# Attention scores and FFN on one core: five passes of scores a slot in place of six, with fill work between the runs and the product with v behind them

## The chip, the core and the metric

The kernel runs on one core of one Trainium2 chip. The metric is the device time of one execution in microseconds (us). The engines are named as in the profile: PE is TensorE's matmuls and PEld its weight loads, DVE is VectorE, ACT is ScalarE, POOL is GpSimd, SP is SyncE. "L515" is line 515 of the kernel before.

## What is computed

One transformer layer on x of shape 2 x 1024 x 512 (float32): a layer norm and attention of 32 heads of width 16, then a layer norm and a feed-forward part with quantised activations and weights (512 to 1376 to 512), each with a residual. The part that the change touches is the attention:

```python
q, k, v = (proj(w_q), proj(w_k), proj(w_v))          # 2 x 32 heads x 1024 x 16
scores = jnp.einsum('bhqd,bhkd->bhqk', q, k) / jnp.sqrt(jnp.float32(D_K))
attn = jax.nn.softmax(scores, axis=-1)
out = jnp.einsum('bhqk,bhkd->bhqd', attn, v)
```

## The kernel before

**Steps and slots.** The attention is cut into 32 steps. A step is one batch, one half of the queries (512), one group of 128 channels (8 heads) and half of its heads: 4 heads. Each of the 4 heads has its own 32 rows (partitions) of the tiles `kst` (keys) and `qst` (queries), so four matmuls with 32 rows each, one per head, can stand in TensorE side by side on four row groups. A step has 8 slots, one per 128 keys (for the exponentials) or per 128 queries and half of the keys (for the maxima). The main loop runs over slots, `T`, and in each slot three different steps are at work: the maxima of the step `nm`, the exponentials of an earlier step `ne` (10 slots behind), and the product with v of the slot before (`nw`).

**Two kinds of scores.** Scores are computed twice. For the maxima (`max_mm`, L475) queries are the stationary side; two passes `l` = 0, 1 (high and low parts of q) accumulate a 128 x 1024 tile `psm` for a pair of heads, and `max_reduce` (L485, DVE) takes the maximum of each row. At the end of a step `max_parts` (L490 to L493, DVE) joins these maxima, and one slot later `max_rows` (L498, PE; L502, ACT) transposes them into `mrow`. For the exponentials (`exp_mm`, L515) keys are the stationary side; two passes give the scores of a pair of heads and a third pass with ones adds the negative maximum from `mrow`; `exponentials` (L519, ACT) then reads this 128 x 1024 tile `pse` and writes `e`. `weigh_values` (L545, PE) multiplies `e` with v into `pso`, and after the last slot of a step copies the sum out (L554, ACT).

**Pairs.** A pair of heads takes two of the four row groups. So the exponentials of the pair 0 (`exps[0]`, row groups 0 and 1) are issued together with the maxima of the pair 1 (`maxs[0]`, row groups 2 and 3), and in the second run the other way round. I call the tiles e0 and m0 (first) and e1 and m1 (second). In a run before the change, `scores` issues e0 alone in the first pass, then e0 with m0, then e0's third pass with m0's second: three passes, of which the first uses two row groups. Two runs make six passes a slot.

**PSUM.** The score tiles `pse` and `psm`, and the transposed maxima `psn`, come from one pool `ps_s` of three buffers, two banks each. The product with v has one bank (`ps_a`), and all other work one bank (`ps_o`). A new tile waits until the reader of the tile that had its buffer is done: ACT for a `pse`, DVE for a `psm`.

**Fill work.** Projections, layer norms and the FFN are generators in the class `Fillers`. In a slot `fill.run(budget)` advances those that are ready until the PE time they name (`("pe", 860.0)`, in ns) reaches the budget: 1300 ns, or 1800 when a projection is near its due slot; what was overdrawn is taken from the next slot (`left`). `("gap", n)` lets a task rest for n calls. A task that needs PSUM asks for the bank with `("take",)`; a bank given back is free from the next call of `run` on. `run(100.0, short=True)` takes only short tasks (the transposes of FFN inputs L780 and of the hidden rows L863). Each call of `run` also advances the "back" tasks, which use no PE: the normalisation of the attention (L571 copy and L572 reciprocal on DVE, L582 on POOL, four DMAs) and the quantisation of the weights. When the loop ends, `turn` works off what is left.

**Order.** The schedule is written by hand: instructions stand in each engine's queue in the order in which the program issues them. In a slot of the kernel before, the order is: run A (e0, m0), product with v of the slot before, short fill, run B (e1, m1), fill. The exponential of a run stands in ACT's queue and the reduction in DVE's queue right behind the run's matmuls, ahead of what the fill issues next.

Of the kernel before, what the change touches and what calls it, by code (L numbers as in the profile page):

```python
# [148 lines left out]
def kernel(  # L149
# [50 lines left out]
    fill = Fillers()  # L200
# [43 lines left out]
    def scores_psum(name):  # L244
        return ps_s.tile([P, 2, QB], F32, tag="s", name=name)
# [201 lines left out]
    def load_k(n):  # L447
        kst[n] = sb.tile([P, S], F32R, tag="kst", name=f"kst_{n}", bufs=3)
        nc.sync.dma_start(kst[n].bitcast(F32), step_k(n))

    def load_q(n):
        b, h, g, s = steps[n]
        qst[n] = []
        for l in range(2):
            q = sb.tile([P, QB], F32R, tag="qst", name=f"qst_{n}_{l}", bufs=6)
            rows = qD[b, g, h][l].rearrange("(r s e) q -> s r e q", r=4, s=2)[s]
            nc.sync.dma_start(q.bitcast(F32), rows)
            qst[n].append(q)

    def load_v(n):  # L460
        b, h, g, s = steps[n]
        vt[n] = sb.tile([P, NT, 4, 32], F32, tag="v", name=f"v_{n}", bufs=2)
        nc.sync.dma_start(vt[n].rearrange("p t r e -> p (t r e)"), vD[b, g, s].rearrange("p t e -> p (t e)"))

    def max_tile(n, i, j):

        if i == 0 and n not in pm:
            pm[n] = sp.tile([P, TQ, 2, 4], F32, tag="pm", name=f"pm_{n}")
        return scores_psum(f"psm_{n}_{i}_{j}")

    def max_mm(n, i, j, ps, l):
        kh, t = divmod(i, TQ)
        for r in (2 * j, 2 * j + 1):
            rows = slice(32 * r, 32 * r + 32)
            nc.tensor.matmul(  # L475
                ps[:, r % 2, :],
                qst[n][l][rows, t * P : (t + 1) * P],
                kst[n][rows, kh * QB : (kh + 1) * QB],
                start=(l == 0),
                stop=(l == 1),  # L480
            )

    def max_reduce(n, i, j, ps):
        kh, t = divmod(i, TQ)
        nc.vector.tensor_reduce(pm[n][:, t, kh, 2 * j : 2 * j + 2], ps, AX.X, ALU.max, negate=True)  # L485

    def max_parts(n):
        m = sp.tile([P, TQ, 4], F32, tag="m", name=f"m_{n}")
        p = pm.pop(n)
        nc.vector.tensor_tensor(m, p[:, :, 0, :], p[:, :, 1, :], ALU.min)  # L490
        cols = mcols[n % 2].rearrange("p t (r c) -> p t r c", r=4)
        nc.vector.tensor_copy(cols[:, :, :, 0], m)
        nc.vector.tensor_tensor(cols[:, :, :, 1], m, cols[:, :, :, 0].bitcast(F32), ALU.subtract)  # L493

    def max_rows(n):
        ps = scores_psum(f"psn_{n}")[:, 0, :]
        for t in range(TQ):
            nc.tensor.matmul(  # L498
                ps[:, t * P : (t + 1) * P], mcols[n % 2][:, t, :], identr, start=True, stop=True
            )  # L500
        mrow[n] = sb.tile([P, QB], F32R, tag="mrow", name=f"mrow_{n}", bufs=2)
        nc.scalar.copy(mrow[n], ps)  # L502
# [3 lines left out]
    def exp_mm(n, i, j, ps, l):  # L506
        for r in (2 * j, 2 * j + 1):
            rows = slice(32 * r, 32 * r + 32)
            if l < 2:
                left, right = kst[n][rows, i * P : (i + 1) * P], qst[n][l][rows, :]  # L510
            else:

                rows = slice(32 * r, 32 * r + 2)
                left, right = onesr[rows, :], mrow[n][rows, :]
            nc.tensor.matmul(ps[:, r % 2, :], left, right, start=(l == 0), stop=(l == 2))  # L515

    def exponentials(n, i, j, ps):
        e = sb.tile([P, 2, QB], F32, tag="e", name=f"e_{n}_{i}_{j}", bufs=4)
        nc.scalar.activation(e, ps, AF.Exp, scale=SCALE)  # L519
        probs.setdefault((n, i), {})[j] = e  # L520

    def scores(exps, maxs):


        es = [(*x, scores_psum(f"pse_{x[0]}_{x[1]}_{x[2]}")) for x in exps]
        ms = [(*x, max_tile(*x)) for x in maxs]
        for l in range(3):
            for x in es:
                exp_mm(*x, l)
            if l or not es:  # L530
                for x in ms:
                    max_mm(*x, l - bool(es)) if l - bool(es) < 2 else None
        for x in es:
            exponentials(*x)
        for x in ms:
            max_reduce(*x)

    acc, po, OT = {}, {}, {}

    def weigh_values(n, i):  # L540
        if i == 0:
            acc[n] = ps_a.tile([P, QB], F32, tag="a", name=f"pso_{n}")
        e = probs.pop((n, i))
        for r in range(4):
            nc.tensor.matmul(  # L545
                acc[n][32 * r : 32 * r + 32, :],
                vt[n][:, i, r, :],
                e[r // 2][:, r % 2, :],
                start=(i == 0),
                stop=(i == NT - 1),  # L550
            )
        if i == NT - 1:
            po[n] = sb.tile([P, QB], F32, tag="po", name=f"po_{n}", bufs=3)
            nc.scalar.copy(po[n], acc[n])  # L554
# [340 lines left out]
    def now(gen):  # L895
        for _ in gen:
            pass
# [80 lines left out]
    NSTEP = len(steps)  # L978
# [23 lines left out]
    def feed():  # L1002

        while ffns and set(ffns[0][2]) <= fill.done | {ffns[0][2][0]}:
            name, gen, after, due = ffns.popleft()
            fill.add(name, gen, after, "ffn", due)


    SHARE, MORE = 1300.0, 1800.0
    left = 0.0  # L1010
    for T in range(LE + NT * NSTEP + 1):
        fill.slot = T
        ne, ie = divmod(T - LE, NT)
        nm, im = divmod(T, NT)
        nw, iw = divmod(T - LE - 1, NT)

        fill.scores = int(T < LE - 1 or T >= NT * NSTEP)

        if (T + 5) % NT == 0 and 1 < (T + 5) // NT < NSTEP:
            n = (T + 5) // NT  # L1020
            b, h, g, s = steps[n]
            fill.ensure(f"k_{b}_{g}_0", f"k_{b}_{g}_1", f"q_{b}_{g}_{h}")
            load_k(n)
            load_q(n)
        if (T - 8) % NT == 0 and 0 <= (T - 8) // NT < NSTEP:
            n = (T - 8) // NT
            b, h, g, s = steps[n]
            fill.ensure(f"v_{b}_{g}_0", f"v_{b}_{g}_1")
            load_v(n)
        if T in (TQ, NT):  # L1030
            fill.ensure(f"first_{T // NT}")
        if im == 0 and 0 < nm <= NSTEP:
            max_parts(nm - 1)
        exps = [(ne, ie, j) for j in range(2)] if 0 <= ne < NSTEP else []
        maxs = [(nm, im, j) for j in (1, 0)] if nm < NSTEP else []
        mixed = bool(exps and maxs)
        if mixed:
            scores(exps[:1], maxs[:1])
        elif exps:
            scores(exps, [])  # L1040
        if 0 <= nw < NSTEP:
            weigh_values(nw, iw)
            if iw == NT - 1 and nw % 2 and nw < NSTEP - 1:
                b, h, g, _ = steps[nw]
                fill.add(f"norm_{b}_{h}_{g}", normalise(nw), (), "back")
        feed()
        fill.run(100.0, short=True)
        if mixed:
            scores(exps[1:], maxs[1:])
        elif maxs:  # L1050
            scores([], maxs)
        if im == 1 and 0 < nm <= NSTEP:
            max_rows(nm - 1)
        share = MORE if fill.urgent() else SHARE
        left = fill.run(min(share + left, share))

    fill.scores = 3
    normalise_last(NSTEP - 1)
# [50 lines left out]
```

## Time and profile before

| | us |
|---|---|
| median of 3 runs | 1315.37 |
| lowest, highest | 1308.07, 1317.15 |
| the profiled execution | 1320.16 |
| its span | 1318.4 |

The span is the time from the first to the last instruction. The page of the profile lists busy time by engine, then groups of instructions by line with the mean of one in ns and the idle time ahead of them. PE's granted clock is 0.965 on the mean. By stretches of the run (us from the start; busy us of each engine):

| stretch | what runs there | PE | DVE | ACT | POOL |
|---|---|---|---|---|---|
| 0 to 121 | norms, first projections, first maxima | 82.7 | 47.8 | 26.1 | 26.2 |
| 121 to 350 | slots, projections, weight quantisation | 214.8 | 161.4 | 131.5 | 107.2 |
| 350 to 1190 | slots, projections, FFN | 823.4 | 603.4 | 500.0 | 111.9 |
| 1190 to 1222 | slots with exponentials alone | 30.2 | 4.5 | 21.9 | 1.3 |
| 1222 to 1318 | last FFN tiles | 58.3 | 49.4 | 32.6 | 0.0 |

An instruction of a group may be short and still decide: what counts is which wait ends last. Ends of matmuls in the profile are modelled, so their starts say more than their durations.

### The profile page before, as it was taken

To read this page: it belongs to the slowest core of one execution; us is meant where nothing else is said; L and a number is where in the kernel's file an instruction comes from. 1 tells how busy PE (TensorE), PEld (TensorE's weight loads), DVE (VectorE), ACT (ScalarE), POOL (GpSimd) and SP (SyncE) were. 2 spreads that over 40 slices of the span, in tenths; PEclk is the share of its full clock that TensorE was granted. 3 is DMA by queue.
4 is the path that set the end of the run, shared out by engine and by line. 5 is a ranking of instruction groups with operands and counts; after the bars stand their busy time and mean duration, and the time that the engine had idled before them with its cause. 6 is when DMAs were issued, how large, how long until landed. Compare 5 with 4: busy or idle time off the path is not lost.

```text
span 1318.4 us, 22143 instructions
## 1 busy us (share of the span) xinstructions
PE 1209.3 (92%) x9082; PEld 541.6 (41%) x9082; DVE 866.5 (66%) x1203; ACT 712.1 (54%) x903; POOL 246.5 (19%) x279
## 2 busy tenths in 40 slices
PE   5768899999999999999999999999999999999566
PEld 2345444334445443444444444444433344443222
DVE  6521468778865667687776676877776867772634
ACT  1124655545655555665666556666665556666243
POOL 1034326455511100321101003110010111100000
PEclk9889999999999999999999999999999979999769
DMA  3056666555333431221213223211133110201000
GB/s 112 0 184 216 225 199 214 156 177 191 126 107 122 136 110 58 89 81 58 72 47 106 95 76 117 76 55 67 57 107 95 58 57 34 82 26 33 24 0 33
DMA packets 72334, 127.88 MB, mean 97 GB/s; under 512 B 9680, under 2 KB 30160, under 8 KB 72232
## 3 DMA queue, kind: packets, MB, share of 16 engines
q1 hardware_dynamic: 64360, 101.16, 23.8%
q0 software_dynamic: 7872, 25.30, 5.9%
q8 instruction: 71, 1.16, 0.4%
q14 instruction: 31, 0.25, 0.1%
HBM read 89.25 MB, written 37.19 MB: 96 GB/s over the span
## 4 chain that ended last, share of the span: by engine, by line
PE 74%; DVE 11%; ACT 5%; issue 4%; DMA 4%; POOL 2%; SPq 0%; ACTq 0%; DVEq 0%; POOLq 0%
PE pse L515 22%; PE pso L545 16%; PE psm L475 8%; PE psy L714 5%; PE psv L418 4%; DVE pm L485 4%; PE psq L351 3%; PE pu L801 3%; PE py L880 3%; PE psk L351 3%; DMA wv<-in_wvT 2%; PE pg L801 2%; ACT e L519 2%; PE psn L498 1%; PE psk L390 1%
## 5 line engine op out<-in xcount | busy, mean ns | idle before, releaser
L485 DVE TENSOR_REDUCE pm<-psm 128x2 f32<-128x1024 f32 x512 | 621.5, 1220 | 336.9 <-PE pse L515 236.8
L519 ACT ACTIVATE e<-pse 128x1024 f32<-128x1024 f32 x512 | 523.0, 1024 | 415.3 <-PE pse L515 315.4
L475 PE MATMUL psm<-kst,qst 32*128 32x512 f32 x2048 | 372.8, 448 | 13.4 <-ACT e L519 8.2
L515 PE MATMUL pse<-qst,kst 32*128 32x512 f32 x2048 | 371.7, 446 | 10.2 <-DVE pm L485 8.8
L515 PEld LDWEIGHTS pse<-qst,kst 32*128 32x128 f32 x2048 | 151.5, 185 | 325.0 <-issue 160.6
L545 PE MATMUL pso<-e,v 128*32 128x512 f32 x2048 | 277.5, 612 | 0.7 <-ACT po L554 0.4
L515 PE MATMUL pse<-mrow,onesr 2*128 2x512 f32 x1024 | 208.6, 406 | 0.0
L475 PEld LDWEIGHTS psm<-kst,qst 32*128 32x128 f32 x2048 | 152.5, 186 | 39.1 <-ACT e L519 27.9
L515 PEld LDWEIGHTS pse<-mrow,onesr 2*128 2x128 f32 x1024 | 95.3, 185 | 5.1 <-ACT mrow L502 0.2
L815 POOL TENSOR_TENSOR g<-g 128x512 f32<-128x512 f32 (+1 forms) x36 | 34.2, 951 | 315.6 <-ACT g L811 315.6
L418 PE MATMUL psv<-wv,xnT 128*128 128x128 f32 x512 | 70.7, 294 | 14.2 <-DMA wv<-in_wvT 12.0
L545 PEld LDWEIGHTS pso<-e,v 128*32 128x32 f32 x2048 | 40.7, 108 | 97.4 <-issue 94.5
L418 PEld LDWEIGHTS psv<-wv,xnT 128*128 128x128 f32 x512 | 64.0, 203 | 27.3 <-issue 19.7
L714 PE MATMUL psy<-wo,OT 128*128 128x512 f32 x128 | 66.7, 635 | 5.9 <-DVE OT L597 5.9
L351 PE MATMUL psq<-xnT,wq 128*128 128x512 f32 x120 | 60.9, 622 | 1.4 <-ACT full_k L359 1.4
L351 PE MATMUL psk<-xnT,wk 128*128 128x512 f32 x112 | 58.4, 640 | 1.5 <-ACT vst L430 1.5
L677 POOL TENSOR_SCALAR low<-raws,whalf 128x512 bf16<-128x512 f32 (+2 forms) x35 | 52.8, 1510 | 21.4 <-DMA raws<-in_wuT 8.5
L801 PEld LDWEIGHTS <-xqT 128*128 128x128 bf16 x384 | 33.1, 102 | 57.5 <-issue 38.0
L770 POOL TENSOR_SCALAR xn<-x,mv,a 128x512 f32<-128x512 f32 x12 | 24.9, 2073 | 166.8 <-DVE a L747 166.7
L801 PE MATMUL pg<-wg,xqT 128*128 128x512 fp8e4 (+1 forms) x192 | 49.9, 387 | 4.0 <-DVE inter L823 2.4
L801 PE MATMUL pu<-wu,xqT 128*128 128x512 fp8e4 (+1 forms) x192 | 47.6, 372 | 3.5 <-ACT g L811 2.5
L880 PE MATMUL py<-wd,iqT 128*128 128x512 fp8e4 (+1 forms) x176 | 45.1, 392 | 2.9 <-ACT g L811 1.7
(124 smaller groups left out, 841.6 us busy)
## 6 DMA issues: line engine op xcount, KB each, us to landing
v<-vD SPq DMA_DIRECT2D x32, 512.0 KB
kst<-kD SPq DMA_DIRECT2D x30, 512.0 KB
qst<-qD SPq DMA_DIRECT2D x60, 256.0 KB
vD<-vst POOLq DMA_DIRECT2D x32, 256.0 KB, 5.4
qD<-hi_q SPq DMA_DIRECT2D x30, 256.0 KB
qD<-lo_q SPq DMA_DIRECT2D x30, 256.0 KB
x<-in_x SPq DMA_DIRECT2D x16, 256.0 KB
wq<-in_wqT SPq DMA_DIRECT2D x16, 256.0 KB
```

Source lines behind the costliest of these rows:

```text
L351: nc.tensor.matmul(ps, w[:, c, :], xnT[b, h][:, c, :], start=(c == 0), stop=(c == KC - 1))
L418: nc.tensor.matmul(ps[:, i * P : (i + 1) * P], xnT[b, half][:, c, i * P : (i + 1) * P], w[:, c, :], start=(c == 0), stop=(c == KC - 1),)
L475: nc.tensor.matmul(ps[:, r % 2, :], qst[n][l][rows, t * P : (t + 1) * P], kst[n][rows, kh * QB : (kh + 1) * QB], start=(l == 0), stop=(l = ...
L485: nc.vector.tensor_reduce(pm[n][:, t, kh, 2 * j : 2 * j + 2], ps, AX.X, ALU.max, negate=True)
L515: nc.tensor.matmul(ps[:, r % 2, :], left, right, start=(l == 0), stop=(l == 2))
L519: nc.scalar.activation(e, ps, AF.Exp, scale=SCALE)
L545: nc.tensor.matmul(acc[n][32 * r : 32 * r + 32, :], vt[n][:, i, r, :], e[r // 2][:, r % 2, :], start=(i == 0), stop=(i == NT - 1),)
L677: nc.gpsimd.tensor_scalar(low, w, h[:rows, m, 1:2], None, ALU.is_lt)
L714: nc.tensor.matmul(ps, OT[b, h, g][:, i * P : (i + 1) * P], wo[g], start=(g == 0), stop=(g == NG - 1),)
L801: nc.tensor.matmul(ps, xT[:, c, :], w[:, c, n : n + size], start=(c == 0), stop=(c == KC - 1))
L815: nc.gpsimd.tensor_tensor(g2[j], g2[j], g2[j], ALU.mult)
L880: nc.tensor.matmul(py, iqT[:rows, c, :], wd[:rows, c, :], start=(c == 0), stop=(c == FC - 1))
```

## The change

`scores` now handles only slots that have exponentials alone or maxima alone. Slots with both use a new generator, `scores_both`. Its first part issues e0 and m0 together in two passes, then e0's third pass together with the first pass of e1, on the row groups that m0 has left; then the exponential of e0 and the reduction of m0. Its second part issues the other two passes of e1 together with both passes of m1. That makes three passes and two.

Between the two parts stands the fill, now in one call with the whole budget; the call for short tasks alone is gone, and short tasks share the budget. Behind the second part come the transposed maxima (when due), then the product with v, then `fill.run(0)`, which advances the "back" tasks and the counter that banks and gaps go by, and issues no PE work of the tasks. The tile e1 is asked for in the first part, ahead of the exponential of e0 and of the reduction of m0; the tile m1 in the second part.

```diff
@@ in scores @@
-            if l or not es:
-                for x in ms:
-                    max_mm(*x, l - bool(es)) if l - bool(es) < 2 else None
+            for x in ms if l < 2 else ():
+                max_mm(*x, l)
...
+    def scores_both(exps, maxs):
+        e0, e1 = exps
+        m0, m1 = maxs
+        p0 = scores_psum(f"pse_{e0[0]}_{e0[1]}_{e0[2]}")
+        q0 = max_tile(*m0)
+        p1 = scores_psum(f"pse_{e1[0]}_{e1[1]}_{e1[2]}")
+        for l in range(2):
+            exp_mm(*e0, p0, l)
+            max_mm(*m0, q0, l)
+        exp_mm(*e0, p0, 2)
+        exp_mm(*e1, p1, 0)
+        exponentials(*e0, p0)
+        max_reduce(*m0, q0)
+        yield
+        q1 = max_tile(*m1)
+        for l in range(2):
+            exp_mm(*e1, p1, l + 1)
+            max_mm(*m1, q1, l)
+        exponentials(*e1, p1)
+        max_reduce(*m1, q1)
...
@@ the main loop @@
-        mixed = bool(exps and maxs)
-        if mixed:
-            scores(exps[:1], maxs[:1])
-        elif exps:
-            scores(exps, [])
+        both = scores_both(exps, maxs) if exps and maxs else None
+        if both:
+            next(both)
+        elif exps or maxs:
+            scores(exps, maxs)
+        feed()
+        share = MORE if fill.urgent() else SHARE
+        left = fill.run(min(share + left, share))
+        if both:
+            now(both)
+        if im == 1 and 0 < nm <= NSTEP:
+            max_rows(nm - 1)
         if 0 <= nw < NSTEP:
             weigh_values(nw, iw)
...
-        feed()
-        fill.run(100.0, short=True)
-        if mixed:
-            scores(exps[1:], maxs[1:])
-        elif maxs:
-            scores([], maxs)
-        if im == 1 and 0 < nm <= NSTEP:
-            max_rows(nm - 1)
-        share = MORE if fill.urgent() else SHARE
-        left = fill.run(min(share + left, share))
+        fill.run(0)
```

## The prediction

> **What bounds the kernel now.** I read the page's busy shares first, then its costliest groups, then the timeline of TensorE (PE) in a steady stretch, and ScalarE (ACT) beside it. One slot of the main loop has two score runs, A and B, the product with v between them and fill work (projections, FFN) after B; 246 slots (T = 10 to 255) hold both exponentials and maxima. Page:
>
> ```profile
> PE 1209.3 (92%) x9082; PEld 541.6 (41%) x9082; DVE 866.5 (66%) x1203; ACT 712.1 (54%) x903; POOL 246.5 (19%) x279
> L485 DVE TENSOR_REDUCE pm<-psm 128x2 f32<-128x1024 f32 x512 | 621.5, 1220 | 336.9 <-PE pse L515 236.8
> L519 ACT ACTIVATE e<-pse 128x1024 f32<-128x1024 f32 x512 | 523.0, 1024 | 415.3 <-PE pse L515 315.4
> ```
>
> PE is the bound. In the stretch from 121 to 1190 us only 30.6 us of its idle time is shown; the rest must be shortened matmuls or waits that the modelled ends cover. VectorE (DVE) waits 336.9 us before its reductions, ACT 415.3 us before its exponentials: both have air. The timeline of PE (start, duration, line) over one slot, run A first:
>
> ```profile
> 702.25 0.50 PE L515 MATMUL pse<-qst,kst 32*128 32x512 f32 x2
> 702.27 0.50 PE L475 MATMUL psm<-kst,qst 32*128 32x512 f32 x2
> 702.59 0.39 PE L515 MATMUL pse<-qst,kst 32*128 32x512 f32 x2
> 702.61 0.39 PE L475 MATMUL psm<-kst,qst 32*128 32x512 f32 x2
> 702.82 0.40 PE L515 MATMUL pse<-mrow,onesr 2*128 2x512 f32 x2
> 703.15 1.07 PE L545 MATMUL pso<-e,v 128*32 128x512 f32 x8
> 704.15 0.50 PE L515 MATMUL pse<-qst,kst 32*128 32x512 f32 x2
> 704.40 0.49 PE L475 MATMUL psm<-kst,qst 32*128 32x512 f32 x2
> 704.49 0.39 PE L515 MATMUL pse<-qst,kst 32*128 32x512 f32 x2
> 704.72 0.40 PE L515 MATMUL pse<-mrow,onesr 2*128 2x512 f32 x2
> 704.74 0.40 PE L475 MATMUL psm<-kst,qst 32*128 32x512 f32 x2
> 705.07 1.12 PE L351 MATMUL psq<-xnT,wq 128*128 128x512 f32 x2
> 706.12 0.50 PE L515 MATMUL pse<-qst,kst 32*128 32x512 f32 x2
> ```
>
> The durations are modelled, so I use starts. A run takes 0.90 to 0.92 us (702.25 to 703.15, 704.15 to 705.07): three passes of the pse chain, 0.34 + 0.23 + 0.33. The two psm passes run beside it on the other two row groups and fit even when their first starts 0.25 us late, as in the second run. Over all 471 such runs, 0.90 us holds up to a lateness of 0.25; beyond that the run lasts the lateness plus 0.65. So two passes cost 0.66 and three 0.90. The last slots have exponentials alone, three passes with all four row groups, and cost no more:
>
> ```profile
> 1204.44 0.74 PE L515 MATMUL pse<-qst,kst 32*128 32x512 f32 x8
> 1205.01 0.41 PE L515 MATMUL pse<-mrow,onesr 2*128 2x512 f32 x4
> 1205.35 1.06 PE L545 MATMUL pso<-e,v 128*32 128x512 f32 x8
> ```
>
> Why is psm late by 0.25? ACT's timeline has the exponential of a run 0.50 us after the start of its last pse pass, hence 0.15 to 0.17 after the run's end:
>
> ```profile
> 703.33 1.02 ACT L519 ACTIVATE e<-pse 128x1024 f32<-128x1024 f32 x1 [0.47 <-PE pse L515]
> ```
>
> It ends at 704.35; psm starts at 704.40. There are three score buffers in PSUM and four tiles a slot, so run B's maxima take the buffer that run A's exponential frees. End of run to free buffer: about 1.22 to 1.25 us, of which the product with v covers 1.00 (703.15 to 704.15).
>
> **What the Trainium skill says.** "TensorEngine Tiling (Array Packing)", Key Properties: row tiles run independently and a change of mode drains the array; the trace agrees (psm 0.02 us after pse, a pass of 0.34 after a change against 0.23). "TensorE: Matmul & The Clock Gate", The mechanism, says matmuls start in program order; here the measurement decides otherwise: psm at 702.27 precedes the second pse pass at 702.59, which stands before it in the program. A wait does hold back what follows: at 1179.59 both the waiting psm and the pse pass behind it start together. "Perfetto Trace Analysis", Optimization Strategy, reads a recurring gap as too few SBUF or PSUM buffers: the 0.25 us here. The same page, on the tensor engine, calls ACT and DVE strict FIFO, and no run of theirs in this trace shows a pass-by.
>
> **The change, part by part.** I take instruction counts and buffers from the two programs as built, and durations from rows.
>
> *Passes.* Run 1 becomes three full passes (0.90), run 2 two (0.66), against 0.90 + 0.91: 0.25 x 246 = **-61.5 us**. Matmuls and weight loads keep their number, 20 each a slot.
>
> *The wait that takes their place.* In the new program the first maxima (m0) take, in 213 of 244 slots, the buffer of the exponential of run 2 just before (e1). Between them is now the product with v alone, 1.00, where it was fill plus the first part of the slot. So m0 starts 0.22 to 0.25 late, as B's maxima did. But its row groups now carry three passes (m0, m0, first pass of e1), so the lateness is no longer covered: run 1 is 0.25 + 0.90 = 1.15. Queued behind the waiting psm are the rest of run 1 and the fill. The slot sums to 1.15 + fill + 0.66 + 1.00 = 2.81 + fill; the old one to 0.90 + 1.00 + 0.91 + fill = 2.81 + fill. Where fill is short, both have a floor near 3.8. In some 30 slots the transposed maxima (L498, 0.50 us) stand between run 2 and run 1 and cover the wait. Cost: 0.25 x 216 = **+54 us**.
>
> *Transposed maxima.* They waited 9.2 us for DVE; their buffer is now that of an exponential long done. **-5**, bounds -9 and 0.
>
> *Fill.* It has one place a slot, and a PSUM bank given back there comes free only after it; the extra short place (PE transposes of 0.28 to 0.55 us) is gone. By the built order the fill in T = 12 to 255 falls from 274 to 260 us; slots with under 0.5 us go from 25 to 44. The shortfall below the 0.99 us that hides a wait sums to 44 us instead of 32. Together **-2**; bounds -14 and +5.
>
> *DVE.* Two waits tighten, both behind the in-order DVE queue. The second maxima (m1) take m0's buffer, so they wait for m0's reduction (1.22) with fill less 0.96 us of slack; the first pass of e1 takes the previous m1's buffer with 0.4 us. Before, the reductions had about 1.8 us until anybody needed them. Now the fill's DVE work stands between the reductions: the |max| of FFN rows (L841, 1.58) in 11 slots, four of them already at the floor: 0.5 each, 6; statistics and inverse roots, 2.2 to 4 us in about 8 slots, 1 to 2 more than before: 9. The copy and reciprocal of the normalisation (L571, 0.78 + 0.34) with the minima (L490 to L493, 0.68) stand ahead of m0's reduction in 14 slots: 0.8 each, 11. A late slot shrinks the next slot's 0.25, some 8 back. **+18**; bounds +5 and +45. ACT's long pieces (L853 1.43 with L811 0.60) delay an exponential by about 1.1 in 11 slots in either program: 0. SP's and POOL's issues keep their order by slot and a share of DMA time under 30% after 350 us; they feed loads due slots later: 0.
>
> *The product with v* moves from between A and B to behind run 2: the same 1.00, its inputs a slot old, the copy of its sum (L554, 0.59) behind e1's exponential instead of ahead: 0, since its bank is next needed a slot later.
>
> *Tail.* When the loop ends, product 10's last part, input 11, product 11 and the output parts of tile 10 are undone that were done before: in the slots with exponentials alone +3, where waits of 0.9 us (ACT) hide part of the added 4.6; after 1222 us, where PE is busy 58 of 96 us at a clock of 0.80, two more output products (about 4 us each) and a start later by some 4 for the DVE work of tile 10: +10. **+13**, bounds +4 and +22.
>
> Sum: -61.5 + 54 - 5 - 2 + 18 + 13 = +16.5. The profiled execution took 1320.16 us (span 1318.4), 4.8 above the median of 1315.37; on the median that is **1332 us**.
>
> **Rivals.** (1) *The wait is hidden*, in whole or large part: exponentials start sooner, or m0's lateness overlaps. For it: eight tenths of -61.5 would then stay; 30 slots surely gain. Against: the exponential follows its pass by 0.50 us in every slot I looked at, and 1.00 of cover is measured. Price: -54 for all, 1278; for half, 1305; I take 1288. It decides where m0's first psm starts under 0.1 us after its pse. (2) *DVE becomes the bound*: with fill near 0.97 in 90 slots m1's slack is nil, every small DVE piece then counts; DVE cost +45 instead of +18: 1359. Against: its 337 us of idle time before reductions. (3) *The passes were never the bound* (row groups already run apart), so nothing is won and the costs stand: 1332 + 7, inside the forecast's range.
>
> **How the numbers follow.** The exchange of pass against wait (with 3): 0.52, own range 1312 to 1350. Hidden wait: 0.30. DVE bound: 0.18. A range of 1288 to 1358 leaves out half of the second and a third of the last. One per cent of the median, about what can be told from no change, is 13 us: faster needs under 1302 (nearly all of the second case), slower over 1328.5 (0.56 of the first, all of the third): 0.27, 0.26, 0.47.
>
> **What would show it.** Run 1 near 1.15 us with psm 0.2 to 0.25 after pse, run 2 near 0.66: the exchange. Run 1 at 0.90: the first rival. More PE idle before L475 and L515 released by L485: the DVE step. The tail after the last exponential longer by about 10. The forecast is wrong if the slot is shorter than 2.7 us plus fill, or if the tail is no longer than now.

## The result, and the profile after

| us | before | after |
|---|---|---|
| median | 1314.58 (4 runs, 1308.07 to 1317.15) | 1334.17 (4 runs, 1332.43 to 1334.77) |
| span of the profiled execution | 1318.4 | 1330.6 |
| from the first slot with exponentials and maxima to the last | 1110.9 | 1123.3 |
| from there to the end | 130.5 | 129.9 |

The ratio is 1.0154, with a 95% interval of 1.0116 to 1.0193: slower by 1.5%, or 19.6 us, where 16.5 were forecast. In the profiled executions the difference arises in the slots. They differ by less than the medians (12.2 us), because the one of the kernel before was longer than its median (1320.16 us) and the one of the changed kernel was its shortest run (1332.43 us). The page after (line numbers behind L525 are 22 higher than before, so L545 is now L567):

```profile
PE 1213.8 (91%) x9082; PEld 532.7 (40%) x9082; DVE 875.5 (66%) x1203; ACT 713.2 (54%) x903; POOL 247.7 (19%) x279
...
PE 72%; DVE 16%; DMA 4%; issue 3%; ACT 2%; SPq 1%; POOL 0%; ACTq 0%; DVEq 0%; POOLq 0%
...
L485 DVE TENSOR_REDUCE pm<-psm 128x2 f32<-128x1024 f32 x512 | 623.5, 1222 | 352.4 <-PE psm L475 276.0
...
L515 PE MATMUL pse<-qst,kst 32*128 32x512 f32 x2048 | 403.1, 452 | 17.8 <-DVE pm L485 17.8
L475 PE MATMUL psm<-kst,qst 32*128 32x512 f32 x2048 | 373.1, 448 | 30.4 <-DVE pm L485 23.7
```

The same lines of the page before, for the chain and for PE:

```profile
PE 74%; DVE 11%; ACT 5%; issue 4%; DMA 4%; POOL 2%; SPq 0%; ACTq 0%; DVEq 0%; POOLq 0%
...
L475 PE MATMUL psm<-kst,qst 32*128 32x512 f32 x2048 | 372.8, 448 | 13.4 <-ACT e L519 8.2
L515 PE MATMUL pse<-qst,kst 32*128 32x512 f32 x2048 | 371.7, 446 | 10.2 <-DVE pm L485 8.8
```

The line of percentages is the chain that ended last by engine: DVE has 16% of it after, 11% before. The last two lines say why: PE now stands idle ahead of score matmuls for DVE's reductions, 17.8 us ahead of pse and 23.7 ahead of psm (before: 8.8 and 3.3; of psm's 13.4 us most were waits for ACT). The counts of matmuls and weight loads are the same, so no work was saved; only the way in which passes lie side by side has changed.

The timeline of PE after (start, duration, line) shows the exchange in two slots. First a slot with one piece of fill:

```profile
727.00 1.07 PE L567 MATMUL pso<-e,v 128*32 128x512 f32 x8
728.00 0.50 PE L515 MATMUL pse<-qst,kst 32*128 32x512 f32 x2
728.03 0.49 PE L475 MATMUL psm<-kst,qst 32*128 32x512 f32 x2
...
728.60 0.39 PE L515 MATMUL pse<-qst,kst 32*128 32x512 f32 x2
728.92 1.04 PE L823 MATMUL pu<-wu,xqT 128*128 128x512 fp8e4 x4
729.89 0.50 PE L515 MATMUL pse<-qst,kst 32*128 32x512 f32 x2
730.08 0.50 PE L475 MATMUL psm<-kst,qst 32*128 32x512 f32 x2
...
730.42 0.40 PE L475 MATMUL psm<-kst,qst 32*128 32x512 f32 x2
730.74 1.07 PE L567 MATMUL pso<-e,v 128*32 128x512 f32 x8
```

Run 1 takes 0.92 us (728.00 to 728.92). In run 2 the first psm stands 0.19 behind the first pse, and the run takes 0.85 in place of 0.66. A slot with two pieces of fill ahead of the product with v:

```profile
735.27 1.06 PE L567 MATMUL pso<-e,v 128*32 128x512 f32 x8
736.27 0.50 PE L515 MATMUL pse<-qst,kst 32*128 32x512 f32 x2
736.52 0.50 PE L475 MATMUL psm<-kst,qst 32*128 32x512 f32 x2
...
737.09 0.41 PE L515 MATMUL pse<-qst,kst 32*128 32x512 f32 x2
737.43 1.98 PE L736 MATMUL psy<-wo,OT 128*128 128x512 f32 x4
```

Here run 1 pays: psm is 0.25 late, e1's first pass (737.09) comes behind the two psm passes on the same row groups, and the run takes 1.16 us. Nearly the same quarter of a microsecond appears in run 1 or in run 2, according to the fill. A small minority of slots pays much more, for DVE. At 781.74 DVE starts the last of a chain of small operations (an inverse root among them), the reduction of the m1 of the slot before comes behind it, and run 1 waits 2.20 us for its buffer:

```profile
780.84 0.40 PE L515 MATMUL pse<-mrow,onesr 2*128 2x512 f32 x2
...
781.74 0.52 DVE L845 TENSOR_TENSOR inter<-pu,g 128x352 f32<-128x352 f32 x1
782.17 1.21 DVE L485 TENSOR_REDUCE pm<-psm 128x2 f32<-128x1024 f32 x1
783.44 0.50 PE L515 MATMUL pse<-qst,kst 32*128 32x512 f32 x2 [2.20 <-DVE pm L485]
```

From the starts of all score runs I took, for each kernel, how late the first psm stood behind the first pse (lateness), and by how much the runs exceed their bare passes, 0.90 us for three and 0.66 for two (paid). These are runs at the full granted clock, with fill or the product with v ahead of them; PE's idle time ahead of the transposed maxima is left out:

| us in all | lateness of psm | paid in the two runs |
|---|---|---|
| before | 40.6 + 50.5 = 91.1 | 15.7 + 16.4 = 32.1 |
| after | 33.8 + 55.0 = 88.8 | 49.8 + 58.0 = 107.8 |

The lateness did not change. Before, a run with a third pass of its own covered 0.25 us of it; after, it is paid in full.

### The profile page after: what moved, and what is told of

It is laid out like the page before. It is cut to its first block, busy times and chain, and to the rows that moved or that the text cites. A ratio compares the mean times of both kernels' runs of the same rounds, so it can differ in the third digit from the quotient of the medians.

```text
span 1330.6 us, 22164 instructions
## 1 busy us (share of the span) xinstructions
PE 1213.8 (91%) x9082; PEld 532.7 (40%) x9082; DVE 875.5 (66%) x1203; ACT 713.2 (54%) x903; POOL 247.7 (19%) x279
## 3 DMA queue, kind: packets, MB, share of 16 engines
q8 instruction: 71, 1.16, 0.4%
## 4 chain that ended last, share of the span: by engine, by line
PE 72%; DVE 16%; DMA 4%; issue 3%; ACT 2%; SPq 1%; POOL 0%; ACTq 0%; DVEq 0%; POOLq 0%
PE pse L515 20%; PE pso L567 16%; PE psm L475 10%; DVE pm L485 8%; PE psy L736 5%; PE psv L418 4%; DMA wv<-in_wvT 4%; PE psq L351 3%; PE psk L351 3%; PE pu L823 3%; PE py L902 3%; PE pg L823 2%; PE psk L390 1%; PE psn L498 1%; PE psq L390 1%
## 5 line engine op out<-in xcount | busy, mean ns | idle before, releaser
L515 PE MATMUL pse<-qst,kst 32*128 32x512 f32 x2048 | 403.1, 452 | 17.8 <-DVE pm L485 17.8
L475 PE MATMUL psm<-kst,qst 32*128 32x512 f32 x2048 | 373.1, 448 | 30.4 <-DVE pm L485 23.7
L515 PEld LDWEIGHTS pse<-qst,kst 32*128 32x128 f32 x2048 | 177.7, 184 | 355.7 <-issue 212.4
L567 PE MATMUL pso<-e,v 128*32 128x512 f32 x2048 | 277.1, 612 | 0.2 <-ACT e L519 0.2
L567 PEld LDWEIGHTS pso<-e,v 128*32 128x32 f32 x2048 | 40.6, 108 | 87.9 <-issue 80.4
L432 POOL DMA_DIRECT2D vD<-vst x32 | 18.1, 567 | 162.3 <-ACT vst L430 162.3
```

The lines of the kernel that those rows point to most:

```text
L475: nc.tensor.matmul(ps[:, r % 2, :], qst[n][l][rows, t * P : (t + 1) * P], kst[n][rows, kh * QB : (kh + 1) * QB], start=(l == 0), stop=(l = ...
L567: nc.tensor.matmul(acc[n][32 * r : 32 * r + 32, :], vt[n][:, i, r, :], e[r // 2][:, r % 2, :], start=(i == 0), stop=(i == NT - 1),)
```

## Experiments

The lengths of runs and stretches below come from the timelines of PE, the medians from the timed runs.

**The order without the packing.** The new order of a slot with the old six passes:

```diff
-        for l in range(2):
-            exp_mm(*e0, p0, l)
-            max_mm(*m0, q0, l)
-        exp_mm(*e0, p0, 2)
-        exp_mm(*e1, p1, 0)
...
+        for e, m in ((e0, m0), (e1, m1)):
+            p = scores_psum(f"pse_{e[0]}_{e[1]}_{e[2]}")
+            q = max_tile(*m)
+            exp_mm(*e, p, 0)
+            for l in range(2):
+                exp_mm(*e, p, l + 1)
+                max_mm(*m, q, l)
...
```

> The new order of a slot (run 1, all fill, run 2, product with v, back tasks) with the old six passes: each run issues its exponentials' first pass alone, so e1 has no pass in run 1. Theory (pass exchanged for wait, DVE slack lost by the packing): run 1 again covers the 0.25 us lateness of m0, slot 2.81 us plus fill as before; the buffers go round in turn and each reduction again has about 1.5 us until it is needed, so the DVE cost (about 18 us of the changed kernel's 20) is gone: 1311 to 1321 us. Rival (the order and the fill's single place cost the time): near the changed kernel, 1328 to 1336. Rival (five passes are worth a pass each): slower than the changed kernel, above 1340.

Measured: 1319.16 us, ratio 1.0028 (1.0009 to 1.0047), in the range of the theory. The lateness is 105.3 us, of which 43.4 are paid. The order with its single place for fill costs 0.3%; the other 1.3% come with the packing. The order may cost some 3 us more at equal clock: these timed runs have about 79 us at a granted clock of 0.5 (half clock), those of the kernel before 89 (what such a microsecond goes with is said in the last section).

**The packing without the order.** `scores_both` in the old order (run 1, product with v, short fill, run 2, fill):

```diff
         if both:
             next(both)
+        if 0 <= nw < NSTEP:
+            weigh_values(nw, iw)
...
+        feed()
+        fill.run(100.0, short=True)
+        if both:
+            now(both)
...
```

> Five passes in the old order (run 1, product with v, short fill, run 2, fill). Theory: run 1 0.90 us, run 2 0.66 plus a lateness of m1 of about 0.21 (its buffer comes from m0's reduction, covered by the product with v alone), so 2.77 us plus fill, 0.04 less than before; but m1 has no slack towards DVE and e1 only that of the fill less 0.88, so DVE work costs 15 to 25 us as in the changed kernel: 1320 to 1332 us. Rival (order is the cause): at or below the kernel before, 1300 to 1315. Rival (passes count in full): 1265 to 1285.

Measured: 1346.84 us, ratio 1.0215 (1.0162 to 1.0267), above my range. The lateness is about 90 us, all of it and more paid (over 100). m1 waits behind the product with v alone for m0's reduction: the runs with two passes pay some 70 us there. In the profiled execution the stretch of slots is 25.8 us longer than before (1136.7 against 1110.9). Some 23 of these lie in the score runs: about 13 in runs at the full clock, the other 10 in runs at half clock and in slots without fill. The timed runs have about 112 us at half clock, the kernel before 89; that this explains why the range was missed is likely, but not shown.

**Less DVE work between the reductions.** The same cut in both kernels; it leaves out most of the row maximum, two of three iterations of the inverse root and most of the merge of sums, so that only times are to be read:

```diff
-        nc.vector.tensor_reduce(gm, v, AX.X, ALU.max, apply_absolute_value=True)
+        nc.vector.tensor_reduce(gm, v[:, :64], AX.X, ALU.max, apply_absolute_value=True)
...
-        for i in range(3):
...
-        nc.vector.copy_predicated(p0, second.to_broadcast([P, QB]), p1)
+        nc.vector.copy_predicated(p0[:, :64], second.to_broadcast([P, 64]), p1[:, :64])
```

> The changed kernel with DVE work left out: the row maximum of the FFN over 64 of 1376 columns, one of three iterations of the inverse root, the merge of the two heads' sums over 64 of 512 columns. Its own gain holds the work that left the tail as well, so it is read against the same cut in the kernel before. Theory (DVE queue ahead of the reductions is what costs): it gains 10 to 15 us more than the old kernel does by the same cut; the two then differ by 5 to 10 us in place of 20. Rival (DVE is not what costs): they still differ by 17 to 23 us.

> The kernel before with the same DVE work left out (row maximum over 64 of 1376 columns, one of three iterations of the inverse root, merge over 64 of 512 columns): the control. Its slack of about 1.8 us per reduction hides most of this work in the slots; the tail loses about 1.5 us for each of the last row maxima: 1300 to 1308 us by either theory.

Measured: 1315.96 us (changed, 20 runs) and 1293.76 us (before, 4 runs). They differ by 22.2 us: the rival's number. Paid in the runs: 99.9 in place of 107.8, and 29.8 in place of 32.1, so this work costs the changed kernel some 6 us more than the old one, not 10 to 15. I expected the control to gain less, too. A part of the difference is clock: the timed runs have 89 us at half clock against 69. In the profiled executions the slots lose 12.8 us in the changed kernel and 18.8 in the old one, so it does not gain more there either. The tail differs too: the cut shortens it from 130.5 to 121.5 us in the old kernel and not in the changed one (129.9, then 133.4). So these DVE operations are not what makes the difference, though each case of a late reduction is real; what the operations that I left in cost was not measured apart.

**Short tasks in a place of their own again**, behind the product with v:

```diff
-        fill.run(0)
+        fill.run(100.0, short=True)
```

> The changed kernel with the extra call for short tasks put back, behind the product with v. The fill then runs as far as before by the end of the loop, and tile 10 and product 11 leave the tail. If moving them cost the tail nothing (they filled waits and kept the clock up), the slots take about 14 us more fill, less 0.25 us in some 24 slots where a transpose stands between the product with v and run 1, and the tail shortens by less than 4 us, its product 12 again at about half clock: 1334 to 1344 us. If the tail had paid for them (some 10 us, as forecast): 1325 to 1333.

Measured: 1336.67 us, ratio 1.0174 (1.0128 to 1.0220), in the first range. The stretch of slots takes 1132.9 us (the changed kernel 1123.3), the tail 128.2 (129.9). By the medians, these runs show no difference from the place of the short tasks.

**The fill split over both places:**

```diff
-        left = fill.run(min(share + left, share))
+        total = min(share + left, share)
+        first = min(total, 860.0) if both else total
+        left = fill.run(first)
...
-        fill.run(0)
+        left = fill.run(left + total - first)
```

> The changed kernel with the slot's fill in two places: up to 860 ns between the runs, the rest behind the product with v. Where a second piece stands there (slots with two pieces or more), m0's lateness of 0.25 us is hidden. Theory: run 1 falls to 0.90 in these 80 to 100 slots, but run 2 then waits for m0's reduction by 0.15, so 0.10 to 0.25 us a slot: 10 to 25 us less than the changed kernel, 1310 to 1325. If m0's wait for e1's exponential is not what run 1 pays for: no change, 1330 to 1338.

Measured: 1384.20 us, ratio 1.0547 (1.0507 to 1.0588): a miss by some 60 us. Where fill stood ahead of run 1, that run did fall to its bare length (some 115 runs, under 5 us over 0.90 in all). But the stretch of slots is 51.6 us longer than in the changed kernel (1174.9 against 1123.3), and most of that is not in the score runs. The fill takes 33 us more: it does 84 more matmuls there, in 339 places in place of 239, and the tail is no shorter for it (131.1 us). The product with v takes 13 us more, most of it at half clock, and the score runs 8. In 33 slots, 8 in the changed kernel, no fill was left between the runs; there both runs together take 3.1 us in place of 1.56, because nothing covers m0's reduction. The time at half clock in the timed runs rose from 96 to 144 us. Why the fill costs so much more in two places was not taken apart.

**Another owner of the buffer.** The three score buffers handed out strictly in turn, so that m1 follows e0 (ACT) and not m0 (DVE); a buffer goes to the end of the row when its reader is issued:

```diff
-        return ps_s.tile([P, 2, QB], F32, tag="s", name=name)
+        k = free_s.popleft()
+        t = ps_s.tile([P, 2, QB], F32, tag=f"s{k}", name=name, bufs=1)
+        tag_of[id(t)] = (k, t)
+        return t
...
```

> The changed kernel with the three score buffers handed out strictly in turn: m1 takes e0's buffer (ACT) instead of m0's (DVE), and e0 takes that of the last m0. Nothing else moves. Theory: the waits of psm for DVE's reductions (20.4 us of idle PE in the changed kernel) go, the waits of pse for m1's reduction (17.8) stay, m0's 0.25 stays: 8 to 15 us less, 1319 to 1327. Rival (it is the order of the queues, not whose buffer): no change, 1330 to 1338.

Measured: 1332.23 us, ratio 1.0149 (1.0101 to 1.0198), no change: the rival's number, and the 8 to 15 us of the theory did not come. Paid: 56.0 + 47.1 = 103.1 us. Run 2 pays 11 us less, run 1 6 more. An exponential (1.02 us) frees a buffer hardly sooner than a reduction (1.22), and three buffers stay three.

**Score tiles read in a quarter.** Exponential and maximum take 128 of each 512 columns, and the product with v uses these four times; the matmuls stay as they are:

```diff
-        nc.vector.tensor_reduce(pm[n][:, t, kh, 2 * j : 2 * j + 2], ps, AX.X, ALU.max, negate=True)
+        nc.vector.tensor_reduce(pm[n][:, t, kh, 2 * j : 2 * j + 2], ps[:, :, :128], AX.X, ALU.max, negate=True)
...
-        nc.scalar.activation(e, ps, AF.Exp, scale=SCALE)
+        nc.scalar.activation(e[:, :, :128], ps[:, :, :128], AF.Exp, scale=SCALE)
```

> The changed kernel with its score tiles read in a quarter: the exponential and the maximum take 128 of each 512 columns, and the product with v uses these columns four times; all matmuls keep their number and size. Each buffer comes free about 0.6 us (ACT) and 0.75 us (DVE) sooner, under the 1.00 us that the product with v covers. Theory (the pass saved is paid back only by lateness of score buffers): the 108 us over the bare passes in the changed kernel fall to under 35, and it ends below the same cut of the kernel before by 35 to 60 us: 1215 to 1240. Rival (packing the passes is worth nothing on TensorE, or the order costs by itself): equal to the cut kernel before or slower.

> The kernel before with the same cut (exponential and maximum on 128 of each 512 columns, product with v on these four times): the control. Of 91 us of lateness its runs pay only about 32, so it has less to gain: 1260 to 1285 by theory and rival.

Measured: 1213.55 us (1212.89 to 1216.52) and 1251.13 us (1248.85 to 1255.55). With buffers freed early, the packed kernel is 37.6 us faster than the old one under the same cut. Both fell a little more than expected, perhaps because shorter reductions and exponentials also leave time for others in their queues. Paid: 8.8 + 7.7 = 16.5 and 1.1 + 5.3 = 6.4 us. In the slots of the profiled executions the packed kernel is 47.3 us shorter (1012.7 against 1060.0); its tail, with more fill left in it, is 5.9 longer. The timeline of PE in the cut changed kernel has the two bare runs:

```profile
708.85 0.49 PE L515 MATMUL pse<-qst,kst 32*128 32x512 f32 x2
708.85 0.50 PE L475 MATMUL psm<-kst,qst 32*128 32x512 f32 x2
...
709.51 1.07 PE L567 MATMUL pso<-e,v 128*32 128x512 f32 x8
710.51 0.50 PE L515 MATMUL pse<-qst,kst 32*128 32x512 f32 x2
710.52 0.49 PE L475 MATMUL psm<-kst,qst 32*128 32x512 f32 x2
```

psm starts 0.00 and 0.01 us behind pse, and run 2 takes 0.66 (708.85 to 709.51). So TensorE does give the pass; late buffers take it back, with the two engines that empty them. This settles the main step.

**Padding in the place of the wait.** Four small matmuls ahead of run 1 in the changed kernel, and at the same place, ahead of run B, in the old one:

```diff
+        for _ in range(4):
+            nc.tensor.matmul(p0[:, 0, :P], identb, identb, start=True, stop=True)
```

> The changed kernel with four extra matmuls of 128x128 (bf16, into the tile that e0 is about to overwrite) ahead of run 1, behind the product with v: 0.22 to 0.28 us a slot, 54 to 69 us in all. Theory: where m0 is late for e1's exponential the padding takes the place of the wait, so about 34 us of it cost nothing: 1352 to 1368. Rival (run 1 does not pay for that wait): the whole of it, 1388 to 1403.

> The kernel before with the same four matmuls at the same place, between the product with v and run B. There the lateness of 0.25 us is covered by the run's own three passes, so by the theory nothing of the padding is hidden but about 8 us of the longer waits: 1360 to 1382, no faster than the padded changed kernel. By the rival too the whole price is paid here.

Measured: 1376.68 us and 1375.95 us. The padding costs more than I had put in, 0.32 us a slot, as the timeline of the padded changed kernel shows:

```profile
703.48 0.40 PE L546 MATMUL pse<-identb 128*128 128x128 bf16 x4
703.80 0.49 PE L515 MATMUL pse<-qst,kst 32*128 32x512 f32 x2
703.81 0.51 PE L475 MATMUL psm<-kst,qst 32*128 32x512 f32 x2
```

That is some 78 us in 244 slots, and psm is hardly late any more (8 us in all in run 1). The old kernel pays 65.1 of them (from 1310.84). The changed kernel without padding was not timed in this series: from 1334.17 it pays 42.5, from the 1331 that its ratio gives beside 1310.84 some 46. So 32 to 35 us are hidden there, near the 34 that run 1's lateness offered, and 13 in the old kernel. The timeline agrees: run 1 pays about 21 us in place of 49.8. Both padded kernels take the same time. My absolute range for the changed one was missed for the price of the padding.

**The clock in the tail.** The kernel before with 40 matmuls put into its long wait ahead of tile 12:

```diff
+        if order == 12:
+            pw = spare("pswarm")
+            for _ in range(40):
+                nc.tensor.matmul(pw, identb, wg[:, 0, :512], start=True, stop=True)
```

> The kernel before with 40 extra matmuls of 128x512 into a spare bank ahead of the transposes of tile 12, in the wait of about 10 us in the tail. If the low granted clock (0.54 in the 22 us that follow) comes from TensorE's idleness there, product 12 runs at full clock and the end comes 4 to 8 us sooner: 1306 to 1311 us. If the clock does not follow the idleness: no change, or up to 2 us later, 1314 to 1318.

Measured: 1310.56 us, ratio 0.9984 (0.9966 to 1.0003). The time lies in the range, but not for my reason, and it is no change beyond its interval. The granted clock was 0.97 from 1225 to 1245 us, around the padding (1232 to 1241), and 0.62 in the 25 us that follow, so product 12 ran slowly all the same. Behind the padding PE pauses again: it is busy 39% of the 3.4 us ahead of that fall. Keeping TensorE busy ahead of its pauses did not hold the clock through them; filling the pauses themselves was not tried. No version that still does all of the layer's work beats the kernel before beyond its interval.

## Why the prediction was right

The forecast of 1332 us stands beside 1334.17. By its terms, with the profiled executions:

| term | forecast | measured |
|---|---|---|
| passes | -61.5 | -57 (0.24 x 238 slots) |
| wait of m0, shortfall of fill, DVE | +54 + 12 + 18 = +84 | +76 paid at full clock |
| score runs at half clock | not forecast | +18 over their bare passes |
| fill moved out of the slots | -14 | -19 |
| transposed maxima | -5 | -9 in PE's idle time ahead of them (9.2 to 0.4), +2.5 in their own time |
| tail | +13 | -0.6 |
| sum | +16.5 | +11 by these rows, +12.2 in the spans, +19.6 in the medians |

The mechanism and the sum of its main terms held. That the whole came out within 3 us is partly luck: the tail was put 14 us too high and the waits 8, and the runs at half clock, which the prediction did not count, brought 18. The rows are those of one execution of each kernel.

- *The exchange of pass against wait* is shown: by the two slots above, by an unchanged lateness that is now paid, by the cut that takes the lateness away and leaves the packed kernel 37.6 us ahead, and by the padding. But the 0.25 us that I had put into run 1 of 216 slots lies in run 1 (33.8 us) and in run 2 (a part of 55.0). Where a single piece of fill stands between the runs, m1's wait for m0's reduction holds run 2 back first (0.18 us in the median), and the next run 1 is then nearly on time (0.07); behind two pieces run 2 is on time (0.01) and the next run 1 late by 0.25. The prediction had priced m1's wait only as short fill and DVE work, and not in these slots. The sum was right, the place was half wrong.
- *Short fill*: 57 slots with under 0.75 us of fill pay 40.7 us in run 2. A shortfall of 44 us was counted, 12 more than before, and it is the largest single piece there.
- *DVE*: the wait of e1's first pass for m1's reduction came as described (24 slots, 28.7 us, half-clock slots included), with the operations that I had named ahead of it. But the cut of these operations brought the changed kernel only about 6 us more than the old one. The +18 was too high for what those operations do alone; how it divides further stays open.
- *The tail* is the term that was mis-sized, and by the prediction's own last sign (a tail no longer than now) the forecast was wrong in it. Product 11 and the output parts of tile 10 did move behind the loop, and PE's busy time there rose from 90.6 to 95.6 us; the tail did not grow. The windows of the tail, before and then after, with product 12 in each (stretch, length, busy us of PE, PEld, DVE, ACT and POOL, granted clock, share of DMA, GB/s):

```profile
1253.00:1275.00 22.00, 15.58 (x44) 5.67 (x45) 6.00 (x13) 7.20 (x13) 0.00 (x0) 0.54 0.00 1
```

```profile
1267.00:1289.00 22.00, 15.95 (x84) 7.33 (x83) 13.18 (x28) 10.58 (x17) 0.00 (x0) 0.92 0.04 13
```

PE gets 84 matmuls done after in the time of 44 before (23 and 8 of them small transposes), at a clock of 0.92 in place of 0.54; in the timeline the matmuls of product 11 stand where PE waits for DVE and ACT before. Over the kernels that I ran, tails with the two tiles in them took 129.9 to 135.8 us, tails without 128.2 to 131.6 (127.3 and 121.5 where exponentials or DVE work were cut): the moved work costs perhaps 4 us, not 13. In the profiled execution of the changed kernel the clock may have given these back: its tail has 17 us at half clock, that of the kernel before 38.

- *The change of mode*: I read the pass of 0.34 us against 0.23 as the drain at a change of tiling. The last pass ahead of a change takes 0.33 as well, and both kinds of kernel have it; that a drain is the reason is shown by no run here.

The rivals: in a third of the slots (80 of 230 at the full clock) run 1 is under 0.95 us, near the 0.90 that I had named as the sign of the first, but there run 2 of the slot before has paid in its place (53 slots) or the transposed maxima cover the wait (24), and over all runs more is paid than the lateness; the wait was not hidden. DVE did not become the bound: cutting its work moved little. That the passes were never the bound, the third, is refuted by the cut that leaves the packed kernel 37.6 us ahead.

## What to carry to other kernels

A group of passes that runs side by side has slack in its shorter chain, and that slack may be what hides a buffer's release. Before filling it, count how long a buffer is away (here the last pass to the next write, about 1.5 us) against the work that stands between, for every buffer in turn. Where the buffers are the bound, as here, packing passes moves time from the matmuls to the waits; shortening what empties the buffers paid in both versions (60 us), and twice as much in the packed one (some 120).

## What I had not expected of the hardware

- In a kernel whose PE is busy 91% of the span, the trace still has periods with a granted clock of 0.5. They last 3.4 us or multiples of it, and no other value than 1 and 0.5 occurs. In the slots behind the first 110 us the profiled kernel before has four (30.7 us in all, 17 of them from 1051 us on), the changed one eight (41.0 us). Each follows 3.4 us in which PE was busy for 11 to 77% of the time; that short pauses bring these periods is likely, but no run tested it alone. A timed run's time at half clock is worked out from its mean clock. Over 39 timed runs of the kernel before (70 to 108 us at half clock each), a run's time rises by about 0.35 us with each such microsecond, and this goes with 59% of the variance between the runs. It is a correlation; if the waits bring the pauses, it adds to the price of a wait.
- Matmuls on other row groups start ahead of earlier ones in the program. This is seen in the kernel before, where the second pse pass (702.59) stands ahead of the first psm pass (702.27) in the program; in the changed kernel the program itself has psm first.
